# A two-layer graph kernel: masks loaded for two steps at once, fourteen tiles by transfers in the last attention, and two queues and stages rearranged

## The chip, the cores and the metric

The kernel runs on one core of a Trainium2 chip. The time is the device time of one execution in microseconds (us), and less is better. Everything is in fp32, with the exception of the masks, which are bytes.

## What is computed

There are N = 4096 nodes with F = 512 features, in H = 4 heads of D = 128. `adj` is a 0/1 matrix of 4096 x 4096, and both patterns of the first layer are this one matrix, so its two softmaxes are the same. Cut to what matters:

```python
# layer 0: encoder attention, MLP, decoder attention (same weights att), MLP
h   = relu(layernorm(x))
Xw  = einsum('hnd,hde->hne', heads(h), W)
sig = sigmoid(f1[:, :, None] + f2[:, None, :])       # f1, f2: Xw times two vectors
att = where(mask, softmax(where(mask, sig, -inf)), 0)
Xn  = batchnorm(einsum('hij,hjd->hid', att, Xw))
emb = batchnorm(elu(Xn @ Wenc.T + b) + Xn)
Yc  = elu(einsum('hij,hjd,hed->hie', att, heads(emb), W))
x   = x + batchnorm(elu(Yc @ Wdec.T + b) + Yc)
# layer 1: one attention with leaky-relu scores
h     = relu(layernorm(x))
feats = einsum('nf,hfo->hno', h, W1)
attn  = softmax(where(A, leaky_relu(e_self[:, :, None] + e_neigh[:, None, :]), -1e10))
out   = x + relu(einsum('hnm,hmo->hno', attn, feats) + b)
```

## The kernel before

**The three attentions.** The function `attention` (L224 to L564) runs three times: the encoder (L739), the decoder (L846) and the last attention (L1088). Each time it goes through eight blocks, four heads times two halves of 2048 targets (`TB`), and each block through 32 steps. A step handles a tile `e` of 128 sources x 2048 targets. ScalarE fills it (L572 tanh and L573 exp in the encoder and decoder, L1051 in the last attention). VectorE multiplies it by its mask (L574; L1052). Then TensorE accumulates four products of 128 x 128 by 128 x 512 into four banks (L470; in the step `EVICT` = 2 the fourth bank catches up, L467). The decoder handles six pairs of steps with seven products in place of eight (`seven`, L345, and L332). A fifth of the masked tiles is kept in DRAM by the encoder (`ekeep`) and read back by the decoder, which needs no denominators. `weight_tile` (L255) hands out the buffers of `e`: two of one pool and 6, 5 or 7 of another (`ebufs`).

**Denominators.** The encoder and the last attention need the sum of `e` over its sources. Three ways share the 32 tiles of a block, by the tables of L62 to L70, each a pair of `moved` and `by_ones`:

- `moved` tiles are added by the DMA engines, in two transfers of 512 KB each, which GpSimd issues (L490): the first of a block writes the target, the others accumulate. The target is `acc2`, or `w` and `R` in the last attention. The trace names these transfers `acc<-e` and `w<-e`.
- `by_ones` tiles go through TensorE: four products with a stationary of ones of 32 columns, straight into the bank `den` (L268).
- the rest VectorE adds (L498, L500, and L504 for the last six tiles of the last block).

At the end of a block TensorE reduces VectorE's sum with four such products (L517), and the moved sum with four more (L515). A third entry, `ends_later`, puts the latter into step 1 of the following block (L528, seen as `den<-w`). The inner six blocks of the last attention use `GAT`, the outer two `GAT_FIRST` and `GAT_LAST`. In the very last block the products of the last four steps are held back (`late`, L476) until `den` is done, and then L538 and the output follow.

**The end of a block** is spread over the steps of the following one by `ending` (L300): `denominators` copies `den` and writes four rows of it to DRAM (`dens`), `columns` reads them back in another shape (`dcol`), `invert_them` inverts, `inverses` writes them (`rinvs`), and `spread` reads each part back for all partitions (`rb`). The queue of these transfers is `hop` (L263): GpSimd in the encoder and decoder, ScalarE in the last attention. `slack` is 4 steps after encoder block 0, otherwise 0 (L526).

**Masks.** At the start GpSimd issues eight casts of `adjT` from fp32 to bytes, 1024 sources x 2048 targets each (`copy_adjacency`, L600), into DRAM tiles `masks[t][g]` (L166). Every step loads its own mask of 256 KB on SP's queue (L426 to L430, `load_mask` L211) into one of five buffers (L209). The first five are loaded ahead of the encoder (L673). A decoder step whose `e` is read back loads none.

**From the second MLP to the last attention.** `mlp_block` (L747) ends with the product `last_product`. While the statistics of its last feature block are finished, TensorE works on four groups of small products (L903), each followed by a product that serves only to keep it busy (`stay_busy`, L117, which reads `w0Ts`, a table held from the start, L129). `residual` (L866) adds x to a block of 512 nodes: ScalarE scales, VectorE adds. `centred` (L910) takes the mean over features by a product with a constant matrix (`mean_of`; for block 0 it is split into the sum of three feature blocks, L919, and the fourth, L920), subtracts it (L931, four times), and makes relu (`hT`, L935) and squares for the variance (L938 to L940). `values` (L951) multiplies `hT` by the layer's weights, eight products per 128 nodes (L957); `deviation` (L943) gives the scale. Two groups of 128 nodes of block 0 run ahead of it (L964).

**Order.** A scheduler places the instructions of each engine in the order of the program, except where `tc.issue_after` and `pinned` put one behind another, `at(j, ...)` puts work into step j of the following block, and `extras` into named steps.

Of the kernel before, what the change touches and what calls it, by code (L numbers as in the profile page):

```python
# [31 lines left out]
FP = mybir.dt.float32  # L32
U8 = mybir.dt.uint8
# [7 lines left out]
IB = 512  # L41
# [23 lines left out]
ENC = (0, 2, 5, 7, 10, 12, 15, 17, 20, 22, 25), (8, 9, 30, 31)  # L65

GAT_FIRST = (0, 2, 4, 6, 8, 10, 12, 14, 16, 18, 20, 22, 24), (30, 31)
GAT = tuple(range(3, 28, 2)), (31,), True

GAT_LAST = (3, 5, 7, 9, 11, 13, 15, 17, 19, 21, 23), (28, 29, 30, 31)  # L70

# [19 lines left out]
def kernel(ctx, tc, x, xT, adjT, w0, w0T, v0, wencT, wdecT, vecs, w1, w1T, a1, outT):  # L91
# [25 lines left out]
    def stay_busy(behind, n=1, cols=IB):  # L117

        for _ in range(n):
            with tc.issue_after(behind.ins):  # L120
                behind = nc.tensor.matmul(bank()[:, 0:cols], ident, w0Ts.rearrange("p h d -> p (h d)")[:, 0:cols],
                                          start=True, stop=True)
        return behind

# [1 line left out]
    make_identity(nc, ident)  # L126
    ones = consts.tile([P, P], FP, name="ones")
    nc.gpsimd.memset(ones, 1.0)
    w0Ts = consts.tile([P, H, D], FP, name="w0Ts")  # L129
    nc.scalar.dma_start(w0Ts, w0T)  # L130
    vec = consts.tile([P, len(VECS), 4], FP, name="vec")
    nc.scalar.dma_start(vec, vecs)

# [29 lines left out]
    ekeep = [[[dram.tile([P, TB], FP, name=f"ekeep{h}_{t}_{k}") for k in range(NJ // KEEP)] for t in range(NTB)]  # L163
             for h in range(H)]

    masks = [[dram.tile([MG * P, TB], U8, name=f"mask{t}_{g}") for g in range(NJ // MG)] for t in range(NTB)]  # L166

    def everywhere(d, row, lo, n):

# [36 lines left out]
        return nc.sync.dma_start(rowb, everywhere(d, row, 0, TB))  # L206

    def mask_tile(keep):
        return keep.tile([P, TB], U8, name="a", bufs=5)  # L209

    def load_mask(a, tb, j):  # L211

        return nc.sync.dma_start(a, masks[tb][j // MG][(j % MG) * P:(j % MG + 1) * P, :])

    @contextmanager
    def pinned(behind):
# [7 lines left out]
    def attention(what, keep, pools, weights, values, row_of, out, finish, ebufs, modes=None, invert=None,  # L224
# [43 lines left out]
                last_ones = nc.tensor.matmul(den[s * 32:(s + 1) * 32, :], ones[:, 0:32], t[:, s * IB:(s + 1) * IB],  # L268
                                             start=start, stop=stop)

        def denominators(h, tb, den):

            dsb = spool.tile([P, IB], FP, name="dsb", tag="rb", bufs=3)
            (nc.vector.tensor_copy if kept is not None else nc.scalar.copy)(dsb, den)
            hop.dma_start(dens[h][tb], dsb[0:P:32, :])

        def columns(h, tb, dcols):

            dcol = spool.tile([P, TB // P], FP, name="dcol", bufs=2)
            hop.dma_start(dcol, dens[h][tb].rearrange("s (q k) -> (s q) k", k=TB // P))  # L280
            dcols.append(dcol)
# [18 lines left out]
        def ending(h, tb, po, den, slack):  # L300

            outs = [out(spool, h, tb, s, po[s]) for s in range(SB)]
            if den is not None:

                dcols = []
                at(INVERT, denominators, h, tb, den)
                at(INVERT + (0 if hop is nc.gpsimd else 3), columns, h, tb, dcols)
                at(INVERT + slack + (6 if hop is nc.gpsimd else 7), invert_them, dcols)
                at(INVERT + slack + (6 if hop is nc.gpsimd else 10), inverses, h, tb, dcols)
            rbs = {}  # L310
            for s, o in enumerate(outs):
# [84 lines left out]
        for n, (h, tb) in enumerate(blocks):  # L396
# [10 lines left out]
                if tb == 0:  # L407
                    fast[2](h)
            ahead, late = [], []
            adds, held, stores, at_end, next_row = [], [], [], [], None  # L410
            for j in range(NJ):

                with pinned(products_of):
# [9 lines left out]
                if store and kept == "read":  # L423
                    a_load = nc.sync.dma_start(e, ekeep[h][tb][j // KEEP])
                else:
                    if masks0:  # L426
                        a, a_load = masks0.pop(0)
                    else:
                        a = mask_tile(keep)
                        a_load = load_mask(a, tb, j)  # L430

                    with pinned([*(products_of[:1] if kept == "read" and n == 0 and j < 8 else ()),
                                 *(behind if n == 0 and j < EP else ())]):
                        products_of = weights(e, rowb, a, j, h, SB if NJ * n + j < in_parts0 else 1)
# [144 lines left out]
    with tc.tile_pool(name="keep", bufs=1) as keep:  # L579

        with tc.tile_pool(name="f_small", bufs=1) as small, tc.tile_pool(name="f_work", bufs=2) as work:
            xs = []
            w0x = small.tile([P, H, DX], FP, name="w0x")
            v0s = small.tile([P, H, 2], FP, name="v0s")
            nc.scalar.dma_start(v0s, v0)
            nc.scalar.dma_start(w0x[:, :, 0:D], w0)
            for ib in range(NIB):
# [12 lines left out]
            def copy_adjacency(n, behind):  # L600

                t, g = divmod(n, NJ // MG)
                cast = nc.gpsimd.dma_start(masks[t][g], adjT[g * MG * P:(g + 1) * MG * P, t * TB:(t + 1) * TB])
                tc.add_manual_dep(cast.ins, behind.ins.name,
                                  mybir.DependencyInfo(mybir.DependencyClass.Sync, mybir.DependencyReason.DATA),
                                  reason="others first")

            for ib in range(NIB):
# [59 lines left out]
                if ib == SB - 1:  # L668
                    store_rows(rows[0], targets(0))
                    row0 = keep.tile([P, TB], FP, name="rowb", bufs=2)  # L670
                    row0_load = load_row(row0, rows[0], 0)
                    with tc.issue_after(row0_load.ins):
                        masks0 = []  # L673
                        for j in range(5):
                            a = mask_tile(keep)
                            masks0.append((a, load_mask(a, 0, j)))
            store_rows(rows[1], targets(1))
# [100 lines left out]

        with tc.tile_pool(name="m_small", bufs=1) as small, tc.tile_pool(name="m_work", bufs=3) as work:
            yc = [R[3]] + [small.tile([P, N], FP, name=f"yc{o}") for o in range(1, C)]  # L780

            def last_head():
                bn_coefs(stats, "enc_bn_gamma", "enc_bn_beta", a_att, b_att, C - 1, C)
# [67 lines left out]
    v1 = xd  # L851

    edge = ctx.enter_context(tc.tile_pool(name="edge", bufs=1))
    jcol = edge.tile([P, NTB, H, NJ // NTB], FP, name="jcol")
    jcol2 = edge.tile([P, NTB, H, NJ // NTB], FP, name="jcol2")
    nq = edge.tile([P, NTB, H, NJ // NTB], FP, name="nq")
    with tc.tile_pool(name="l_small", bufs=1) as small, tc.tile_pool(name="l_work", bufs=2) as work:
# [5 lines left out]
        a1s = small.tile([P, H, 2], FP, name="a1s")  # L863
        nc.scalar.dma_start(a1s, a1)

        def residual(o, ib):  # L866
            d = nodes(x1[o], ib)
            xt = work.tile([P, IB], FP, name="xt")
            nc.sync.dma_start(xt, xT[o * P:(o + 1) * P, ib * IB:(ib + 1) * IB])
            nc.scalar.activation(d, d, AF.Identity, bias=b_mlp[:, o:o + 1], scale=a_mlp[:, o:o + 1])  # L870
            added = nc.vector.tensor_add(d, d, xt)
            if o == 1:
                nc.gpsimd.tensor_add(S[ib], nodes(x1[0], ib), d)
            elif o == C - 2 or o == C - 1 and ib > 0:
# [20 lines left out]
        for fb in range(C):  # L895
            nc.scalar.dma_start(w1x[:, fb, :, 0:D], w1[fb * P:(fb + 1) * P, :].rearrange("p (h d) -> p h d", d=D))
        pw = bank1()
        last_pe = last_product
        for fb in range(C):
            with tc.issue_after(last_pe.ins):  # L900
                for h in range(H):
                    k = 2 * (fb * H + h)
                    last_pe = nc.tensor.matmul(pw[:, k:k + 2], w1Ts[:, h, fb * P:(fb + 1) * P], a1s[:, h, :],  # L903
                                               start=True, stop=True)
            last_pe = stay_busy(last_pe)
        mean_of = small.tile([P, P], FP, name="mean_of")
        nc.gpsimd.memset(mean_of, 1.0 / F)
        vacc = edge.tile([P, H, D], FP, name="vacc")

        def centred(ib):  # L910

            if ib >= NIB // 2:
                residual(C - 2, ib)
            added = residual(C - 1, ib)
            pm = bank()
            if ib == 0:

                with tc.issue_after(last_pe.ins):
                    nc.tensor.matmul(pm, mean_of, S[ib], start=True, stop=False)  # L919
                nc.tensor.matmul(pm, mean_of, nodes(x1[C - 1], ib), start=False, stop=True)  # L920
                with tc.issue_after(added.ins):
                    nc.vector.tensor_copy(w1x[:, :, :, D:DX],
                                          pw[:, 0:2 * C * H].rearrange("p (c h s) -> p c h s", h=H, s=2))
            else:
                nc.tensor.matmul(pm, mean_of, S[ib], start=True, stop=True)
            hT = work.tile([P, C, IB], FP, name="hT")
            sq = work.tile([P, C, IB], FP, name="sq", bufs=1)

            d = hT if ib else sq
            for fb in range(C):  # L930
                nc.vector.tensor_sub(d[:, fb, :], nodes(x1[fb], ib), pm)  # L931
            for fb in range(C):
                if ib:
                    nc.scalar.activation(sq[:, fb, :], d[:, fb, :], AF.Square)
                last_relu = nc.scalar.activation(hT[:, fb, :], d[:, fb, :], AF.Relu)  # L935
            if ib == 0:
                for fb in range(C):
                    nc.scalar.activation(sq[:, fb, :], d[:, fb, :], AF.Square)  # L938
# [196 lines left out]
```

## Time and profile before

| | us |
|---|---|
| median of three runs | 3187.92 |
| lowest and highest | 3186.09, 3189.45 |
| profiled execution | 3189.23 |
| its span on the core | 3187.4 |
| encoder blocks, start to start on TensorE | 134.5, 126.2, 116.9, 116.4, 118.2, 118.2, 118.1 |
| last product of the second MLP (L724) ends | 2127.76 |
| first product of the values (L957) starts | 2137.93 |
| last attention, blocks start to start on TensorE | 117.2, 111.9, 113.1, 113.1, 113.2, 113.1, 113.1 |
| last attention, block 7 starts | 3066.1 |

| transfer | queue of | count | KB each | us from issue to landing, median |
|---|---|---|---|---|
| `a<-mask` | SP | 720 | 256 | 4.2 |
| `w<-e` | GpSimd | 178 | 512 | 6.5 |
| `acc<-e` | GpSimd | 142 | 512 | 6.9 |
| `mask<-in_adjT` | GpSimd | 8 | 2048 | 107.3 |

The profile is of one execution. Its engines are PE (TensorE), PEld (TensorE's weight loads), DVE (VectorE), ACT (ScalarE), POOL (GpSimd) and SP, the sync engine, which here only issues transfers. The mean clock granted to TensorE was 0.998 of full speed. Times within the execution count from the start of the span; 1.8 us of the execution lie outside it. A line such as `DVE e L574 <- DMA a<-mask: 12.1, 10, 3.0` says that VectorE's instructions of line 574 stood idle for 12.1 us in all, 10 times, 3.0 at most, until the transfer `a<-mask` came in. In the chain of waits a row is a time, a duration and what was running. Fused names such as `R<-R,e` tell the output and the inputs; `acc` lives in a tile of `R` in the last attention.

### The profile page before, as it was taken

Reading aid. Unit: us, or ns where it says so; the run is one execution under the profiler, and the core shown is the slowest. Engines: PE = TensorE matmul, PEld = TensorE weight load, DVE = VectorE, ACT = ScalarE, POOL = GpSimd, SP = SyncE. Lnnn points to the kernel's source line nnn. Section 1 sums busy time; section 2 is a strip of 40 time slices with the busy share of each in tenths; the row PEclk is TensorE's granted clock in tenths of the full one; section 3 lists DMA queues with packets and bytes.
Section 4 is the critical chain, followed back from the end, with each engine's and each line's share of the span. In section 5 each row is a group of like instructions: output and inputs, shape, how many; then the busy total and the mean of one; then the engine's idle time right before and its main releaser. Section 6 shows DMA issues by size and latency. Waiting matters only on the chain.

```text
span 3187.4 us, 30095 instructions
## 1 busy us (share of the span) xinstructions
PE 3140.5 (99%) x10555; PEld 1371.4 (43%) x10555; DVE 2934.3 (92%) x2222; ACT 2572.8 (81%) x1825; POOL 522.3 (16%) x679
## 2 busy tenths in 40 slices
PE   7999999999999999999999999999999999999999
PEld 6334444444444463333333333458644444444444
DVE  7989999999998778999999999785699999999998
ACT  7999999999998449999999999456755666665663
POOL 3001211211211000010100100026312222122221
PEclk9999999999999999999999999999999999999999
DMA  9998978988987014444445454331579999999996
GB/s 212 199 194 252 265 209 232 269 222 228 267 227 205 20 44 149 155 155 159 159 162 165 145 169 145 90 112 57 158 189 232 214 225 237 218 216 236 230 210 174
DMA packets 215488, 590.30 MB, mean 185 GB/s; under 512 B 25928, under 2 KB 29288, under 8 KB 199336
## 3 DMA queue, kind: packets, MB, share of 16 engines
q0 software_dynamic: 70976, 231.94, 38.1%
q1 hardware_dynamic: 132344, 332.53, 30.4%
q10 hardware_dynamic: 12016, 23.90, 2.1%
q8 instruction: 83, 1.36, 0.2%
q14 instruction: 69, 0.57, 0.1%
HBM read 379.20 MB, written 84.30 MB: 145 GB/s over the span
## 4 chain that ended last, share of the span: by engine, by line
PE 73%; DVE 10%; ACT 7%; issue 7%; DMA 2%; DVEq 0%; ACTq 0%; POOL 0%; POOLq 0%
PE ps L470 32%; PE ps L332 22%; PE ps L724 7%; ACT e L572 4%; DVE e L574 4%; PE den L332 3%; PE ps L957 3%; DVE acc L500 3%; ACT e L573 2%; PE den L268 2%; DMA a<-mask 1%; DVE R L500 1%; DVE e L1052 1%; PE ps L806 1%; PE ps L467 1%
## 5 line engine op out<-in xcount | busy, mean ns | idle before, releaser
L470 PE MATMUL ps<-e,R 128*128 128x512 f32 x3992 | 1736.0, 595 | 22.5 <-DVE e L574 18.5
L470 PEld LDWEIGHTS ps<-e,R 128*128 128x128 f32 x3992 | 754.3, 190 | 1000.4 <-issue 924.0
L574 DVE TENSOR_TENSOR e<-e,a 128x2048 f32<-128x2048 f32 (+1 forms) x470 | 1049.6, 2261 | 77.7 <-ACT e L573 64.3
L572 ACT ACTIVATE e<-rowb,score 128x2048 f32<-128x2048 f32 (+1 forms) x470 | 909.0, 1969 | 20.2 <-PE ps L332 9.0
L573 ACT ACTIVATE e<-e 128x2048 f32<-128x2048 f32 (+1 forms) x470 | 866.6, 1879 | 8.3 <-DVE e L574 5.0
L332 PE MATMUL ps<-e,R 128*64 128x512 f32 x2624 | 746.8, 592 | 1.6 <-DVE e L574 1.5
L1051 ACT ACTIVATE e<-rowb,nq,jcol 128x2048 f32<-128x2048 f32 x224 | 459.3, 2088 | 264.1 <-DMA w<-e 137.1
L1052 DVE SCALAR_TENSOR_TENSOR e<-e,jcol,a 128x2048 f32<-128x2048 f32 (+1 forms) x265 | 591.2, 2262 | 2.8 <-ACT e L1051 2.8
L332 PEld LDWEIGHTS ps<-e,R 128*64 128x64 f32 x2624 | 241.9, 137 | 319.8 <-issue 316.2
L500 DVE TENSOR_TENSOR R<-R,e 128x2048 f32<-128x2048 f32 x124 | 282.2, 2276 | 0.0
L500 DVE TENSOR_TENSOR acc<-acc,e 128x2048 f32<-128x2048 f32 x122 | 278.6, 2284 | 1.0
L490 POOL DMA_DIRECT2D w<-e x178 | 149.1, 847 | 610.7 <-DMA w<-e 301.0
L724 PE MATMUL ps<-R,w 128*128 128x512 f32 x512 | 220.8, 592 | 0.6 <-DVE w L698 0.6
L490 POOL DMA_DIRECT2D acc<-e x142 | 119.1, 895 | 517.7 <-DMA acc<-e 199.1
L724 PEld LDWEIGHTS ps<-R,w 128*128 128x128 f32 x512 | 97.1, 190 | 123.0 <-issue 116.5
L332 PE MATMUL den<-e,R 128*64 128x512 f32 x320 | 149.8, 592 | 0.0
L332 PE MATMUL ps<-e,w 128*64 128x512 f32 x288 | 138.1, 592 | 0.7 <-DVE e L574 0.7
L293 POOL DMA_DIRECT2D rb<-rinvs x60 | 34.2, 573 | 519.3 <-DVE R L688 455.2
L957 PE MATMUL ps<-w1x,hT 128*128 128x260 f32 x512 | 115.5, 384 | 1.4 <-ACT hT L935 1.4
L332 PE MATMUL ps<-t,w 128*64 128x512 f32 x336 | 111.2, 592 | 1.0 <-DVE t L341 1.0
L957 PEld LDWEIGHTS ps<-w1x,hT 128*128 128x128 f32 x512 | 96.5, 190 | 19.9 <-issue 3.3
L332 PE MATMUL ps<-t,R 128*64 128x512 f32 x192 | 90.2, 592 | 0.0
(206 smaller groups left out, 2112.9 us busy)
## 6 DMA issues: line engine op xcount, KB each, us to landing
a<-mask SPq DMA_DIRECT2D x720, 256.0 KB, 4.2
w<-e POOLq DMA_DIRECT2D x178, 512.0 KB, 6.5
acc<-e POOLq DMA_DIRECT2D x142, 512.0 KB, 6.9
e<-ekeep SPq DMA_DIRECT2D x48, 1024.0 KB, 5.0
ekeep<-e SPq DMA_DIRECT2D x36, 1024.0 KB, 7.5
mask<-in_adjT POOLq DMA_DIRECT2D x8, 2048.0 KB, 107.3
rowb<-rows SPq DMA_DIRECT2D x16, 1024.0 KB, 7.2
rb<-rinvs POOLq DMA_DIRECT2D x60, 256.0 KB, 4.2
```

The costliest lines, as they stand in the source:

```text
L268: last_ones = nc.tensor.matmul(den[s * 32:(s + 1) * 32, :], ones[:, 0:32], t[:, s * IB:(s + 1) * IB], start=start, stop=stop)
L332: last_half = nc.tensor.matmul(b[g * HD:(g + 1) * HD, :], weight, x, start=start, stop=stop)
L470: last_main = nc.tensor.matmul(b, block(values[h], j), e[:, s * IB:(s + 1) * IB], start=(j == 0), stop=(j == NJ - 1))
L490: nc.gpsimd.dma_start(into_half, e_half, **({"accum_op": ALU.add} if j > moved[0] else {}))
L500: nc.vector.tensor_add(acc, acc, e)
L572: nc.scalar.activation(e, rowb, AF.Tanh, bias=column(score[:, 1], j, h), scale=0.5)
L573: last_act = nc.scalar.activation(e, e, AF.Exp, scale=0.5)
L574: last_dve = nc.vector.tensor_mul(e, e, a)
L724: last = nc.tensor.matmul(z, w[:, fb, o * P:(o + 1) * P], nodes(src[fb], ib), start=(fb == 0), stop=(fb == C - 1))
L957: m = nc.tensor.matmul(banks[k][:, 0:2 * DX], hT[:, fb, c * P:(c + 1) * P], w1x[:, fb, 2 * k:2 * k + 2, :].rearrange("p h x -> p (h x)"), ...
L1051: last_act = nc.scalar.activation(e, rowb, AF.Relu, bias=column(nq, j, h), scale=column(jcol, j, h))
L1052: last_dve = nc.vector.scalar_tensor_tensor(e, e, column(jcol2, j, h), a, ALU.add, ALU.mult)
```

## The change

**The last attention's tables.** The inner blocks add the 14 odd tiles 3 to 29 by transfers and none by ones; before it was the 13 odd tiles 3 to 27, with tile 31 by ones. The two outer blocks stay.

**Masks.** Two steps share one transfer. The DRAM tiles are laid out with a partition's eight rows side by side, and the casts write them so. A buffer holds two steps' masks and there are three, six steps in all (before: five). Three pairs are loaded ahead of the encoder. In a whole run there are 384 transfers of 512 KB for 720 of 256 KB. The decoder now loads both masks of a pair of which it uses one.

**Denominators of encoder block 0.** `dens` and `dcol`, the first two transfers of that block's end, are issued on SP's queue, not on GpSimd's, and `columns` comes two steps later. All other blocks and transfers stay as they are.

**Values in parts.** For block 0 the scale, the addition of x, the product of L920, the subtractions and relu are made for 128 columns first, then for the other 384. The product of L919 moves up to where the first of the four `stay_busy` products was.

**w0Ts.** It is no longer held throughout, but loaded twice, for the first stage and for the first MLP. `stay_busy` reads a tile `filler` instead, which GpSimd sets to ones.

The diff, cut to its core:

```diff
@@ tables
 GAT_FIRST = (0, 2, 4, 6, 8, 10, 12, 14, 16, 18, 20, 22, 24), (30, 31)
-GAT = tuple(range(3, 28, 2)), (31,), True
+GAT = tuple(range(3, 30, 2)), (), True
@@ stay_busy
-                behind = nc.tensor.matmul(bank()[:, 0:cols], ident, w0Ts.rearrange("p h d -> p (h d)")[:, 0:cols],
+                behind = nc.tensor.matmul(bank()[:, 0:cols], ident, filler[:, 0:cols],
@@ w0Ts, called in the first stage and at the head of the first MLP
-    w0Ts = consts.tile([P, H, D], FP, name="w0Ts")
-    nc.scalar.dma_start(w0Ts, w0T)
+    def load_w0T(pool):
+        w0Ts = pool.tile([P, H, D], FP, name="w0Ts")
+        nc.scalar.dma_start(w0Ts, w0T)
+        return w0Ts
@@ masks
-    masks = [[dram.tile([MG * P, TB], U8, name=f"mask{t}_{g}") for g in range(NJ // MG)] for t in range(NTB)]
+    masks = [[dram.tile([P, MG * TB], U8, name=f"mask{t}_{g}") for g in range(NJ // MG)] for t in range(NTB)]
...
-        return keep.tile([P, TB], U8, name="a", bufs=5)
+        return keep.tile([P, 2 * TB], U8, name="a", bufs=3)
...
-        return nc.sync.dma_start(a, masks[tb][j // MG][(j % MG) * P:(j % MG + 1) * P, :])
+        k = j % MG // 2
+        return nc.sync.dma_start(a, masks[tb][j // MG][:, k * 2 * TB:(k + 1) * 2 * TB])
@@ attention, ending
-                at(INVERT, denominators, h, tb, den)
-                at(INVERT + (0 if hop is nc.gpsimd else 3), columns, h, tb, dcols)
+                at(INVERT, denominators, h, tb, den, nc.sync if slack else hop)
+                at(INVERT + (0 if hop is nc.gpsimd else 3) + slack // 2, columns, h, tb, dcols, nc.sync if slack else hop)
@@ attention, step j
-                    if masks0:
-                        a, a_load = masks0.pop(0)
-                    else:
-                        a = mask_tile(keep)
-                        a_load = load_mask(a, tb, j)
+                    if two_masks[0] != j // 2:
+                        if masks0:
+                            two, a_load = masks0.pop(0)
+                        else:
+                            two = mask_tile(keep)
+                            a_load = load_mask(two, tb, j)
+                        two_masks = j // 2, two
+                    a = two_masks[1][:, j % 2 * TB:(j % 2 + 1) * TB]
@@ copy_adjacency
-                cast = nc.gpsimd.dma_start(masks[t][g], adjT[g * MG * P:(g + 1) * MG * P, t * TB:(t + 1) * TB])
+                rows_of = adjT[g * MG * P:(g + 1) * MG * P, t * TB:(t + 1) * TB]
+                cast = nc.gpsimd.dma_start(masks[t][g].rearrange("p (m i) -> p m i", i=TB),
+                                           rows_of.rearrange("(m p) i -> p m i", p=P))
@@ first masks
-                        for j in range(5):
+                        for j in range(0, 6, 2):
@@ the edge pool
+    filler = edge.tile([P, IB], FP, name="filler")
+    nc.gpsimd.memset(filler, 1.0)
@@ residual
-        def residual(o, ib):
+        def residual(o, ib, parts=(slice(0, IB),)):
...
-            nc.scalar.activation(d, d, AF.Identity, bias=b_mlp[:, o:o + 1], scale=a_mlp[:, o:o + 1])
-            added = nc.vector.tensor_add(d, d, xt)
+            for p in parts:
+                nc.scalar.activation(d[:, p], d[:, p], AF.Identity, bias=b_mlp[:, o:o + 1], scale=a_mlp[:, o:o + 1])
+                added = nc.vector.tensor_add(d[:, p], d[:, p], xt[:, p])
@@ small products behind the second MLP
+        pm0 = bank()
...
-            last_pe = stay_busy(last_pe)
...
+            if fb == 0:
+                with tc.issue_after(last_pe.ins):
+                    last_pe = nc.tensor.matmul(pm0, mean_of, S[0], start=True, stop=False)
+            else:
+                last_pe = stay_busy(last_pe)
@@ centred
-            added = residual(C - 1, ib)
-            pm = bank()
+            parts = (slice(0, IB),) if ib else (slice(0, P), slice(P, IB))
+            added = residual(C - 1, ib, parts)
             if ib == 0:
+                pm = pm0
                 with tc.issue_after(last_pe.ins):
-                    nc.tensor.matmul(pm, mean_of, S[ib], start=True, stop=False)
-                nc.tensor.matmul(pm, mean_of, nodes(x1[C - 1], ib), start=False, stop=True)
+                    for p in parts:
+                        nc.tensor.matmul(pm[:, p], mean_of, nodes(x1[C - 1], ib)[:, p], start=False,
+                                         stop=(p.stop == IB))
...
-            for fb in range(C):
-                nc.vector.tensor_sub(d[:, fb, :], nodes(x1[fb], ib), pm)
-            for fb in range(C):
-                if ib:
-                    nc.scalar.activation(sq[:, fb, :], d[:, fb, :], AF.Square)
-                last_relu = nc.scalar.activation(hT[:, fb, :], d[:, fb, :], AF.Relu)
+            for p in parts:
+                for fb in range(C):
+                    nc.vector.tensor_sub(d[:, fb, p], nodes(x1[fb], ib)[:, p], pm[:, p])
+                for fb in range(C):
+                    if ib:
+                        nc.scalar.activation(sq[:, fb, :], d[:, fb, :], AF.Square)
+                    last_relu = nc.scalar.activation(hT[:, fb, p], d[:, fb, p], AF.Relu)
```

More of the change, by code (lines that the diff above doesn't have):

```diff
@@ L269, in add_to_den, with denominators @@
                                              start=start, stop=stop)
-        def denominators(h, tb, den):
+        def denominators(h, tb, den, hop):
             dsb = spool.tile([P, IB], FP, name="dsb", tag="rb", bufs=3)
@@ L275, in denominators, with columns @@
             hop.dma_start(dens[h][tb], dsb[0:P:32, :])
-        def columns(h, tb, dcols):
+        def columns(h, tb, dcols, hop):
             dcol = spool.tile([P, TB // P], FP, name="dcol", bufs=2)
@@ L409, in attention @@
             ahead, late = [], []
-            adds, held, stores, at_end, next_row = [], [], [], [], None
+            adds, held, stores, at_end, next_row, two_masks = [], [], [], [], None, (None, None)
             for j in range(NJ):
@@ L584 @@
             v0s = small.tile([P, H, 2], FP, name="v0s")
+            w0Ts = load_w0T(small)
             nc.scalar.dma_start(v0s, v0)
@@ L780 @@
             yc = [R[3]] + [small.tile([P, N], FP, name=f"yc{o}") for o in range(1, C)]
+            w0Ts = load_w0T(small)
             def last_head():
@@ L897 @@
         pw = bank1()
+        pm0 = bank()
+        mean_of = small.tile([P, P], FP, name="mean_of")
+        nc.gpsimd.memset(mean_of, 1.0 / F)
         last_pe = last_product
@@ L904 @@
                                                start=True, stop=True)
-            last_pe = stay_busy(last_pe)
-        mean_of = small.tile([P, P], FP, name="mean_of")
-        nc.gpsimd.memset(mean_of, 1.0 / F)
+            if fb == 0:
[3 more added lines that the diff above has]
+                last_pe = stay_busy(last_pe)
         vacc = edge.tile([P, H, D], FP, name="vacc")
@@ L924, in centred @@
             else:
+                pm = bank()
                 nc.tensor.matmul(pm, mean_of, S[ib], start=True, stop=True)
```

## The prediction

> **What bounds the kernel now.** I read the page first: engines, then the chain. TensorE is busy almost throughout, so the page alone can't say what a microsecond is worth in a stage; VectorE and ScalarE are near full too.
>
> ```profile
> PE 3140.5 (99%) x10555; PEld 1371.4 (43%) x10555; DVE 2934.3 (92%) x2222; ACT 2572.8 (81%) x1825; POOL 522.3 (16%) x679
> ...
> PE 73%; DVE 10%; ACT 7%; issue 7%; DMA 2%; DVEq 0%; ACTq 0%; POOL 0%; POOLq 0%
> ```
>
> So I asked for stretches of one attention block each (columns: window, length, busy PE, PEld, DVE, ACT, POOL, clock, DMA share, GB/s). Encoder blocks 0, 1 and 4, then two inner blocks of the last attention:
>
> ```profile
> 64.50:199.00 134.50, 123.28 (x344) 49.77 (x344) 123.33 (x60) 133.34 (x73) 0.00 (x0) 1.00 1.05 193
> 199.00:325.20 126.20, 122.39 (x340) 50.68 (x336) 118.07 (x67) 119.71 (x66) 16.04 (x22) 0.99 0.92 225
> ...
> 558.50:676.70 118.20, 116.57 (x309) 49.51 (x305) 114.35 (x64) 118.20 (x65) 22.30 (x30) 1.00 0.90 240
> ...
> 2498.75:2611.86 113.11, 113.11 (x284) 49.05 (x288) 113.11 (x56) 71.55 (x43) 25.28 (x30) 1.00 0.95 224
> 2611.86:2724.97 113.11, 113.11 (x284) 49.05 (x288) 113.11 (x56) 72.38 (x43) 25.23 (x30) 1.00 0.96 225
> ```
>
> Three things are to be seen. In the encoder ScalarE is the engine without a gap: from block 2 on its busy time is the block's length. Its two activations start 1.893 and 1.800 us apart, 32 x 3.693 = 118.2 us, which is block 4. Only blocks 0 and 1 have ScalarE idle. In the last attention PE and DVE both have no gap in six blocks. And DMA is at 0.95 there, 1.05 in block 0, where the eight casts of the adjacency run.
>
> Waits within 64 to 330 us, and the chain of the same stretch:
>
> ```profile
> POOL dcol L280 <- DMA dens<-dsb: 37.3, 1, 37.3
> ...
> DVE e L574 <- DMA a<-mask: 12.1, 10, 3.0
> ACT e L573 <- DVE e L574: 5.0, 3, 3.1
> ...
> DVE dcol L284 <- DMA dcol<-dens: 2.9, 1, 2.9
> ACT e L572 <- PE den L268: 2.5, 3, 1.1
> ```
>
> ```profile
> 146.06 21.29 DMA a<-mask
> ...
> 207.22 37.32 issue
> 244.56 3.08 DMA dcol<-dens
> ```
>
> Masks and the first block's denominators hold VectorE up, and through the e buffers ScalarE: 5.0 + 2.5 = 7.5 us of ScalarE idle, all that the encoder has.
>
> The end of the last attention, VectorE above, TensorE below; and the chain where the values begin:
>
> ```profile
> 3161.53 4.60 DVE L504 TENSOR_TENSOR R<-R,e 128x2048 f32<-128x2048 f32 x2
> 3167.92 1.04 PE L268 MATMUL den<-R,ones 128*32 128x512 f32 x8
> ```
>
> ```profile
> 2135.63 0.87 PE ps L920 x2
> 2136.53 0.70 DVE sq L931
> 2137.25 0.64 ACT hT L935
> 2137.93 7.31 PE ps L957 x32
> ```
>
> VectorE's last add ends at 3166.13, TensorE wants the sum at 3167.92: 1.79 us of slack, no more.
>
> [...] from 100 to 180 us there are 2402 mask packets (2048 B, 96 ns) beside 2818 cast packets (322 ns). [...] GpSimd issued `dens` at 206.6 us and it landed at 244.3, just after the last cast (243.9). [...] four ones products take 0.93 us, while one main product takes 0.858. [...]
>
> **Part 1, ones out (L68).** Removed: four products of tile 31 in each of the six inner blocks. Two rows of den products (x16) take 1.85 us, so 0.93 each: 6 x 0.93 = 5.5 us of TensorE. VectorE's work is unchanged: 13 moved + 1 by ones before, 14 moved now, 18 tiles (17 adds) either way; tile 29 leaves its adds and 31 enters. VectorE in an inner block, by distance of starts: 32 x 2.263 + 17 x 2.202 + 4 x 0.602 + 0.24 = 112.5 us; TensorE 113.11, now 112.18. The trace gives TensorE a lead to eat: e was ready 3.6 us ahead at its least in block 1, growing 0.7 per block; now it shrinks 0.2 to 0.3 per block, to about 2.3, so no stall within blocks. But in the last block VectorE has the last word: it has no gap from 2285 to 3166, so its last add stays at 3166.13 after the stage's start, and TensorE's product of R can move only from 3167.92 to 3166.2. **Worth 1.7 us, not 5.5**; 3.8 us come back as a wait on L504. Bounds: 5.5 if VectorE got faster somewhere, 0 if a transfer delays it.
>
> Moved in: six tiles of two 512 KB accumulations. The 13th tile's last half landed at 2609.0, 2720.4, ... 3056.2, and TensorE reads w (L528's `den<-w`) at 2616.4, 2729.5, ... 3068.9. The 14th takes some 5.6 us more (its e was ready at 2595, so only the earlier half's landing holds it). Landing about 2614.6, 2726 against 2614.6, 2726.8 (TensorE earlier by 0.93 per block). A wait of up to a microsecond in an early block eats from the 3.8 that TensorE has to spare: 0. Queued behind it on GpSimd: `out<-R` and the next block's first accumulation, which wait for `den<-w` now (14 us). ScalarE finishes e 4 us or more ahead of VectorE throughout, so late buffers have that cover.
>
> **Part 2, two masks in one transfer.** 720 transfers of 256 KB become 384 of 512 KB; packets of 4096 B. From 96 ns at 2048 B and 328 at 8192 B I estimate 173, twice 96 is the other end. Under the casts an engine gives a mask 8 packets x (322 + 96) = 3.3 us at best; counted, 18.8 loads in 80 us, 4.26 us each, where ScalarE wants one per 3.69. Now 8 x (322 + 190) = 4.1 us for two steps. The waits of VectorE on masks (12.1 us) should go. Lookahead stays: the third buffer is free four steps ahead, as the fifth was. In the last attention bytes are equal; engine time falls by 0 to 3 us of 26 per block, against 256 x 326 ns / 16 = 5.2 us added. Decoder: 48 x 256 KB more, at a DMA share of 0.44 to 0.49: nothing. First mask of the last attention: landed at 2267.65, used at 2268.9; 512 KB lands some 0.7 later: 0 to 0.3. Casts write the same 2048 B runs, only spread: 0.
>
> **Part 3, denominators of encoder block 0 on SP.** `dens` and `dcol` no longer stand behind the casts; VectorE's wait of 2.9 (L284) goes, and GpSimd's accumulations needn't queue behind a 37 us wait. Added waits on SP: `dens` for L274, `dcol` for `dens`. Behind them on SP is the mask pair of steps 10 and 11, which VectorE wants some 16 us later. A quiet queue lands such a transfer in 3 to 4 us (`dcol<-dens`, 3.5): no stall. Had it the 15 to 17 us that masks took here, it would be one.
>
> Parts 2 and 3 together: ScalarE's 7.5 us of idle. TensorE has 119.8 and 119.1 us of work in blocks 0 and 1 (128 x 0.858, and 10 ones tiles) against ScalarE's 118.2, and eight e buffers take up the 2.5 us difference and the start. What may stay: the e of step 12 is held until its accumulation gets through behind the casts. Ends 2 and 7.5; **I take 6.0**.
>
> **Part 4, values in parts.** L919 takes a filler's place earlier: -0.93 ahead of the pair. Then 128 columns suffice to begin: x by 0.2 us less at least, L920 0.22 for 0.87, [...] L935 0.27 (as L987) for 0.57. From the last product at 2127.76: 4 x 0.79 + 0.86 + 3 x 0.96 = 2134.7, + 0.4 + 0.2 + 0.3, first value at 2135.7 instead of 2137.93: 2.2. Squares end about 1.1 us earlier (2140.5), S by 2143.0, when the two blocks of values end too. Ends 1.0 and 2.3; **I take 2.1**. If ScalarE's eight small activations take longer than thought, it is late for the second block of values, and 1 us goes.
>
> **Other.** Second `w0Ts` load: ACT issues it after 1042.7; its table load then has until 1049.9, 5.9 us of cover; 0.3 if it waited for L688's last. Filler memset: GpSimd is 16% busy. 0.
>
> **Sum:** 6.0 + 2.1 + 1.7 = 9.8 us. The profiled execution took 3189.23 (span 3187.4, 1.8 around it), 1.3 above the median of 3187.92: 3179.4 by it, 3178.1 by the median. I forecast **3178**. A measurement of this kernel tells about 0.2% (6.4 us) from no change: faster is below 3181.5, slower above 3194.3.
>
> **Rivals.** (B) The encoder's gain is mostly hidden: accumulations behind the casts (244 us) still hold e, 1.5 instead of 6.0: **3182.5**. For it: 0.92 DMA share in block 1; against: the chain names masks and dens, not `acc<-e`. (C) Ones worth their full 5.5: **3174**; against it, VectorE's gapless row. (D) Slower: the accumulations become the bound of the last attention. First issue to last landing is 102.6 us for 13 tiles (2617.8 to 2720.4), 108.2 for 14, and 1.4 from `den<-w` to the next issue: 109.6 of VectorE's 112.4. From 0.2 us more per tile on (7.9 now), blocks stretch; at 5% more (0.4 us), 14 x 0.4 - 2.8 = 2.8 x 6 = 17 us, less the 8 gained elsewhere: **3197**. For it: 0.957 + 5.2/113 = 1.00 DMA share; against: block 0 had 1.05, and mask packets halve. (E) SP stands 15 us behind `dens`, and VectorE waits some 7 us: **3185**.
>
> **Chances:** main 0.55, B 0.20, C 0.10, D 0.08, E 0.07. Faster: nearly all of the main case, C, and under half of B, 0.71; slower D, 0.08; within 0.2% the rest, 0.21. Range 3174 (C) to 3185 (E); outside lie D and a few tails. The main case alone: 3175.5 to 3181.
>
> **What would show it.** Right: no ScalarE gap over 0.5 us from 64 to 325; `dens` landing within 5 us; blocks 0 and 1 together 6 us shorter; values beginning 2 us sooner; in the last attention VectorE still gapless, and a new PE wait of 3 to 4 us on L504 at the end. Wrong: VectorE gaps in the last attention, ACT waits on `w<-e` reaching VectorE, or PE waits at `den<-w` adding to more than 4 us.

## The result, and the profile after

The changed kernel takes 3196.15 us (median of 8 runs, 3190.78 to 3203.5), the kernel before 3187.89 in the same runs (3186.02 to 3189.45): a ratio of 1.0026, with a 95% interval from 1.0018 to 1.0035. It is slower by 8.3 us, where I forecast 9.8 us less. The runs of the changed kernel also lie further apart, 12.7 us against 3.4. Its profiled execution took 3193.98 (span 3192.2), 2.2 below its median, and the one of before 1.3 above; so the two traces are 4.8 us apart, not 8.3, and what follows from them is said of these two executions.

The page: engines, the chain that ended last, and transfers (queue, count, KB each, median us from issue to landing).

```profile
PE 3138.2 (98%) x10507; PEld 1369.8 (43%) x10507; DVE 2933.6 (92%) x2227; ACT 2573.8 (81%) x1830; POOL 530.4 (17%) x690
...
PE 52%; DVE 16%; issue 14%; DMA 11%; ACT 6%; POOL 1%; DVEq 0%; ACTq 0%; SPq 0%; POOLq 0%
...
a<-mask SPq DMA_DIRECT2D x384, 512.0 KB, 5.1
w<-e POOLq DMA_DIRECT2D x190, 512.0 KB, 7.2
acc<-e POOLq DMA_DIRECT2D x142, 512.0 KB, 7.6
```

PE, DVE and ACT have as much work as before, within 2.3 us. What is new is DMA in the chain, 11% for 2%. And the accumulations, which the diff doesn't touch, take longer to land: 7.2 for 6.5 us (`w<-e`), 7.6 for 6.9 (`acc<-e`).

The same stretches as before, of the changed kernel: encoder blocks 0, 1 and 4, then inner blocks 2 to 4 of the last attention (all by VectorE's starts).

```profile
63.20:185.70 122.50, 116.74 (x310) 48.15 (x311) 118.48 (x58) 122.37 (x68) 0.00 (x0) 0.99 1.05 195
185.70:311.00 125.30, 120.06 (x329) 49.84 (x328) 114.67 (x64) 123.88 (x68) 14.28 (x19) 1.00 0.99 235
545.50:665.90 120.40, 116.83 (x304) 49.43 (x304) 114.51 (x64) 118.55 (x65) 22.11 (x29) 1.00 0.87 236
2485.60:2598.30 112.70, 109.31 (x260) 47.05 (x259) 112.43 (x57) 70.52 (x41) 26.72 (x32) 0.98 0.99 233
2598.30:2713.40 115.10, 115.10 (x280) 50.01 (x279) 112.45 (x56) 70.54 (x41) 26.70 (x32) 1.00 0.97 228
2713.40:2829.90 116.50, 112.27 (x265) 48.11 (x264) 112.48 (x56) 70.84 (x41) 26.75 (x32) 0.97 0.97 227
```

(Columns as in the prediction.) By VectorE's starts, encoder blocks 0 and 1 took 128.4 and 124.6 us before and take 122.5 and 125.3. Block 4 took 118.2 and takes 120.4: a new loss. In the last attention the blocks were 112.4 apart; blocks 2 to 5 now take 112.7, 115.1, 116.5 and 115.7, with VectorE's work 112.4 to 112.5. From the first mask product of that stage to the last it was 892.7 us and is 902.6. That is a loss of 9.9 us.

The chain through it (start, duration, what ran), and two waits of the inner blocks (in all, times, longest):

```profile
2486.35 7.01 DMA w<-e
...
2493.65 7.34 DMA w<-e
...
2501.03 1.07 PE den L272 x4
...
2508.22 103.00 PE ps L477 x240
2611.22 1.04 PE den L272 x8
...
2612.28 0.04 DVE R L505
```

```profile
PE den L272 <- DMA w<-e: 7.6, 4, 2.8
...
DVE R L505 <- PE den L272: 5.9, 2, 3.3
```

Block 1's last accumulation lands at 2501.0. TensorE had wanted `w` since 2496.6 and stood idle for 3.4 us in two pieces. By the prediction's sum it has 112.18 us of work per block for VectorE's 112.4, so it catches up hardly at all. A block later its reduction of `R` comes 2.65 us too late for VectorE's first sum, which overwrites `R` (L505). So VectorE, which sets the pace of the stage, waits. The same happened two blocks later (TensorE 4.2 us, VectorE 3.3), and in between VectorE lost 4.0 us on an `e` that came late: ScalarE's queue stood 5.3 us behind the issue of `dcol`, for `dens`, which follows TensorE's late product of `w`. VectorE's waits, 2.65 + 4.0 + 3.3, are the 9.9 us.

### The profile page after: what moved, and what is told of

Same layout as the page of the kernel before. It is cut to its first block, busy times and chain, and to the rows that moved or that the text cites. A ratio compares the mean times of both kernels' runs of the same rounds, so it can differ in the third digit from the quotient of the medians.

```text
span 3192.2 us, 29192 instructions
## 1 busy us (share of the span) xinstructions
PE 3138.2 (98%) x10507; PEld 1369.8 (43%) x10507; DVE 2933.6 (92%) x2227; ACT 2573.8 (81%) x1830; POOL 530.4 (17%) x690
## 4 chain that ended last, share of the span: by engine, by line
PE 52%; DVE 16%; issue 14%; DMA 11%; ACT 6%; POOL 1%; DVEq 0%; ACTq 0%; SPq 0%; POOLq 0%
PE ps L336 22%; PE ps L477 13%; PE ps L734 6%; DVE e L1074 5%; DMA acc<-e 4%; DMA w<-e 4%; DVE R L507 4%; ACT e L579 3%; PE den L336 3%; PE ps L979 3%; DVE e L581 3%; DVE acc L507 2%; ACT e L580 2%; DMA rinvs<-dcol 1%; PE ps L817 1%
## 5 line engine op out<-in xcount | busy, mean ns | idle before, releaser
L497 POOL DMA_DIRECT2D w<-e x190 | 158.5, 843 | 608.4 <-DMA w<-e 364.8
L336 PE MATMUL ps<-t,w 128*64 128x512 f32 x336 | 111.3, 592 | 1.1 <-DVE t L345 1.1
```

The lines of the kernel that those rows point to most:

```text
L336: last_half = nc.tensor.matmul(b[g * HD:(g + 1) * HD, :], weight, x, start=start, stop=stop)
L497: nc.gpsimd.dma_start(into_half, e_half, **({"accum_op": ALU.add} if j > moved[0] else {}))
```

## The experiments

There were two theories at first. **A**: the fourteenth tile makes the chain of accumulations longer than VectorE's block (rival D of the prediction). **B**: the mask pairs slow the accumulations. The expectations after the first four runs split B: **P**, the longer packets; **U**, two masks at once (bunching); **L**, the layout in DRAM. "Before" is the kernel before, timed beside the run.

| kernel | median | before | ratio, 95% interval |
|---|---|---|---|
| changed | 3196.15 | 3187.89 | 1.0026, 1.0018 to 1.0035 |
| e1 changed, old table | 3190.83 | 3187.89 | 1.0009, 1.0001 to 1.0018 |
| e2 only table | 3185.78 | 3187.89 | 0.9993, 0.9985 to 1.0001 |
| e3 only pairs | 3194.98 | 3187.89 | 1.0023, 1.0014 to 1.0032 |
| e4 ones left out | 3186.49 | 3187.89 | 0.9993, 0.9985 to 1.0001 |
| e5 pairs by two loads | 3194.43 | 3187.52 | 1.0021, 1.0012 to 1.0029 |
| e6 pairs in a row | 3240.92 | 3187.52 | 1.0168, 1.0154 to 1.0182 |
| e7 only layout | 3188.03 | 3187.22 | 1.0001, 0.9993 to 1.0009 |
| e8 only denominators | 3194.21 | 3187.52 | 1.0020, 1.0012 to 1.0028 |
| e9 only values | 3185.27 | 3187.22 | 0.9994, 0.9987 to 1.0000 |
| e10 changed, single masks | 3190.73 | 3187.52 | 1.0012, 1.0005 to 1.0018 |
| e11 pairs first, then single | 3182.29 | 3187.22 | 0.9985, 0.9977 to 0.9992 |
| e12 pairs in a row again | 3225.72 | 3187.40 | 1.0120, 1.0106 to 1.0133 |
| e13 pairs in the encoder | 3186.05 | 3187.40 | 0.9996, 0.9988 to 1.0004 |

### Which part costs: e1 to e4

e1 is the changed kernel with the old line 68.

> The changed kernel with the last attention's old table (13 tiles by transfers, tile 31 by ones). Theory A, the fourteenth tile makes the chain of accumulations longer than VectorE's 112.4 us per block: the stall of the last attention is gone, VectorE's blocks 112.4 us apart again, and the gains before it stay (4.6 us up to the end of the second MLP, 1.5 in the values): 3181 to 3183 us. Theory B, the mask pairs slow the accumulations: blocks 3 to 5 of the last attention still take 114 to 116 us, 3190 us or more.

e2 is the kernel before with the new line 68.

> The kernel before with the new table alone (14 tiles by transfers, none by ones, single masks). Theory A: the last attention loses 8 to 14 us as in the changed kernel, 3196 to 3202 us. Theory B: accumulations keep their pace of 7.9 us per tile, 3186 to 3188 us.

e3 has the hunks on masks, casts and `w0Ts` alone.

> The kernel before with mask pairs alone (three buffers of two, casts and first loads to match, the table w0Ts moved to make room). Theory A: some of the encoder's gain, nothing lost later, 3183 to 3187 us. Theory B: the encoder gains as much, but the last attention's accumulations slow down and it loses 5 us or more, 3190 to 3195 us.

e4 keeps 13 transfers and leaves tile 31 of the inner blocks out of the sum:

```diff
-                        held.append(e)
+                        held.extend([] if ends_later else [e])
```

> The kernel before, but tile 31 of the six inner blocks of the last attention is left out of the denominators: no ones products and no transfer in their place. By the prediction's step (VectorE sets the end, 1.79 us of slack) 5.5 us less TensorE work give 1.7 us, 3186.2 us, with a new wait of TensorE on L504 at the end. The rival, TensorE sets the pace of every block: 5.5 us, 3182.4 us.

Theory A falls as it stood: the table alone (e2) doesn't cost, its point estimate is 2.1 us less. e1 has the blocks of theory A, 112.4 us apart, and the time of theory B. e3 is 7.1 us slower, as B had it, but not where I had put it: with 13 tiles its last attention keeps its 112.4 us too, and it loses its time in the encoder. Both causes are needed in the last attention, as the time from the first issue of an inner block to its last landing shows:

| | block 1 | 2 | 3 | 4 | 5 | 6 |
|---|---|---|---|---|---|---|
| before, 13 tiles, single | 106.1 | 104.3 | 102.6 | 101.8 | 100.7 | 99.1 |
| e1, 13 tiles, pairs | 108.1 | 107.3 | 106.9 | 103.5 | 104.2 | 103.2 |
| e2, 14 tiles, single | 110.8 | 112.8 | 109.6 | 107.5 | 107.9 | 107.2 |
| changed, 14 tiles, pairs | 116.2 | 114.0 | 116.2 | 114.3 | 108.7 | 111.3 |

The next block's accumulations start only after TensorE has read `w`, about 1.4 us after. With 112.4 us for a block, about 111 is the limit. e2 stays at or under it but for one block, where TensorE waited 0.65 us. The changed kernel goes well past it four times, and waited at two of them. On top of e1 the new table costs 5.3 us; on the kernel before it takes 2.1 off.

e4 tests the step "worth 1.7 us, not 5.5". It came out at 1.4, and its interval (0.3 slower to 4.8 faster) leaves out the 5.5. The wait that I had named is there, 2.6 us for the 3 to 4 expected (TensorE, with the idle time before it in brackets):

```profile
3162.89 1.94 PE L268 MATMUL den<-R,ones 128*32 128x512 f32 x8 [2.60 <-DVE R L504]
```

### Why pairs slow the accumulations: e5, e6, e7, e12

e5 loads a pair by two transfers, from the old layout, so with the old packets:

```diff
-        return nc.sync.dma_start(a, masks[tb][j // MG][:, k * 2 * TB:(k + 1) * 2 * TB])
+        for m in range(2):
+            load = nc.sync.dma_start(a[:, m * TB:(m + 1) * TB], masks[tb][j // MG][(2 * k + m) * P:(2 * k + m + 1) * P, :])
+        return load
```

> Mask pairs alone, but each pair loaded by two transfers of 256 KB issued together, with the DRAM layout and the 2048 B packets of before. The accumulations land 6.2 us after issue before and 6.5 to 6.8 with pairs. Theory P, the longer packets hold the accumulations' packets up: 6.2 us again, 3187 to 3190 us. Theory U, two steps' masks at once are the trouble, whatever their packets: 6.5 us or more, and 3194 us or more. Theory L, the layout in DRAM (rows at a stride of 16 KB): as P.

e6 and e12 keep one transfer in 4096 B packets, but lay each pair out in one piece (`[MG // 2 * P, 2 * TB]`), with four casts per group in e6, two in e12:

> Mask pairs alone, one transfer of 512 KB in packets of 4096 B, but each pair contiguous in DRAM (4096 B rows, one after the other; each cast is issued as four). Theory L, the stride of 16 KB is the trouble: accumulations land in 6.2 us, 3184 to 3188 us. Theories P and U: 6.5 us or more, 3193 to 3197 us as with pairs alone.

> Mask pairs alone, one transfer of 512 KB in packets of 4096 B, each pair contiguous in DRAM, with two casts per group and those of the second half of the targets issued after the first stage, so that the encoder should start at about 64 us again. Theory P, the length of the packets is enough: accumulations land in 6.5 us or more and encoder blocks 3 to 7 lose 3 to 6 us together; whole time 3192 to 3197 us if the start isn't late. Theory L, the stride has to come with it: blocks 3 to 7 lose less than 1 us, 3185 to 3189 us.

e7 changes only the layout:

> The kernel before, single masks in 256 KB transfers, only the layout in DRAM changed to the new one (a partition's eight mask rows side by side, so that one mask is 128 rows of 2048 B at a stride of 16 KB) with the casts to match. Theory L, the stride slows the masks and what runs beside them: accumulations land in 6.4 us or more after issue (6.2 before), encoder blocks 3 to 7 lose 2 us or more together, 3190 us or more. Theory P, it is the length of the packets or the bunching of the two masks: 3186 to 3189 us.

The "6.2 us" of these texts is a mean from the end of the issue. Below are the median and the mean from the start of the issue, for encoder blocks 3 to 7 (440 to 1010 us) and the inner blocks of the last attention (2400 to 3050); e6 and e12 by 50 and 36 us later. Beside them stand ScalarE's waits on accumulations, and the time of encoder blocks 3 to 7 together, from VectorE's first mask product to the end of its last (all in us).

| masks there | kernel | encoder: landing, median | mean | ScalarE's waits | blocks 3 to 7 | last attention: landing, median | mean |
|---|---|---|---|---|---|---|---|
| short packets | before, e2, e4, e7 to e11 | 6.7 to 6.9 | 7.1 to 7.2 | 0 to 0.4 | 589.3 to 589.8 | 6.7 to 7.0 | 7.0 to 7.2 |
| short, two at once | e5 | 6.9 | 7.3 | 0 | 589.4 | 6.6 | 7.2 |
| long, in a row | e6, e12 | 7.1, 7.4 | 7.4, 7.4 | 0.4, 1.5 | 589.8, 590.2 | 7.0, 7.1 | 7.3, 7.3 |
| long, at a stride | e1, e3, changed | 7.1 to 7.6 | 7.5 to 7.7 | 3.7 to 4.7 | 592.4 to 594.6 | 7.2 to 7.4 | 7.4 |

Two masks at once don't do it, and the stride with short packets doesn't (e7 is the kernel before within its interval). So P is right that no loss is seen without long packets. That their length is enough is not shown: in a row, the accumulations come later by about half as much, and encoder blocks 3 to 7 lose less than 1 us, which e12's text had set as the outcome of theory L. A loss of 3 us and more is seen only with long packets at a stride. What the stride adds stays open.

The whole times of e6 and e12 say nothing on the pairs, since both kernels started late, at 122 and 91 us for 64: GpSimd, which issues the casts between its share of the first stage, stood idle for 105.7 us in e6 until earlier casts had landed.

The packets allow an estimate. From 2400 to 3050 us a mask packet took 97.9 ns on average before and takes 199.5, the accumulations' packet 331 and 325; the masks' share of the engines is 22.3% in both. The accumulations' 153 transfers of 512 KB before are 19500 packets of 4096 B in that stretch, so about 128 each, 8 for each of the 16 engines on average. If each of these waits for one mask packet at most, 0.10 us more now, the transfer lands at most 8 x 0.10 = 0.8 us later; at a stride it lands 0.2 to 0.6 later on average. That they wait so is my assumption: no run here shows the order of the packets on one engine. And the length can't be all of it, since the mask packets of e6 and e12 are about as long (196.5 and 191.3 ns).

e5 met the number of theory U, 3194, for another reason: its encoder blocks 3 to 7 and its last attention have no loss, its decoder takes 939.4 us for 929.5. VectorE there waits 20.3 us for kept tiles (`e<-ekeep`), which are loaded on the same queue as the masks (1.5 before, 9.7 in the changed kernel, whose decoder takes 929.8). Why the waits grow so in e5 stays open.

### The denominators and the values: e8, e9, e10

> The kernel before with the denominators of encoder block 0 on SP's queue alone. By the prediction's step the wait of 2.9 us on dcol and what stands behind dens on GpSimd goes: ScalarE's idle time from 230 to 290 us falls by 2 to 4 us, 3184 to 3186 us. Rival E: SP's masks stand behind dens, 3190 us or more.

> The kernel before with the values in parts alone. From the last product of the second MLP to the first product of the values 8.0 to 8.6 us instead of 10.1, and 3185.8 to 3186.5 us. If the last attention's start takes it back: 3187.5 us.

> The changed kernel with the single masks of before: new table, denominators of encoder block 0 on SP, values in parts. If the parts add up: 2.1 from the table, 2 to 3 from the denominators, 1.5 from the values, 3181 to 3183 us. If one of them rests on the pairs: 3185 us or more.

With single masks the denominators on SP cost 6.7 us: rival E, to its size. Here are SP's queue in e8, and VectorE's and ScalarE's waits of 195 to 300 us:

```profile
197.10 11.35 SPq L213 DMA_DIRECT2D a<-mask  x4
208.79 0.62 SPq L275 DMA_DIRECT2D dens<-dsb  x1
224.90 0.32 SPq L280 DMA_DIRECT2D dcol<-dens  x1
225.32 13.26 SPq L213 DMA_DIRECT2D a<-mask  x6
```

```profile
DVE e L574 <- DMA a<-mask: 14.0, 5, 8.3
...
ACT e L573 <- DVE e L574: 8.4, 1, 8.4
```

`dens` was issued behind four masks, beside the casts, and SP could issue `dcol` only 16.1 us later. The masks behind `dcol` were issued only then, and VectorE stood 8.3 us for one of them. With pairs (changed kernel) `dens` was issued at 197.7 and `dcol` at 205.5, 7.8 later, and no mask was late. Pairs alone (e3), on the other hand, bring VectorE to `dcol` sooner, and it waits 10.4 us for it. Encoder blocks 0 and 1 took 253.0 us in the profiled execution of before, but 250.4 to 251.0 in those of e2, e4, e7 and e9, whose encoder is that of before (in e7 with the other layout of the masks). Against these, e3 takes 251.5, e8 256.2, and the changed kernel 247.9. So neither half gains alone, the denominators on SP even cost 5 to 6 us, and together they gain about 3.

e10 isn't 3181 to 3183 because of that 8.3 us wait, which is in it too: 6.7 for e8, less 2.1 for e2 and 1.9 for e9, is 2.7, and it is 3.2 us slower. It also has the fourteen tiles with single masks in the five old buffers, and its last attention takes 893.2 us, so the loss there goes with the pairs. e9 is 1.9 us faster (0 to 4 by its interval).

### What each place is worth: e11 and e13

e11 keeps everything but uses pairs only in encoder blocks 0 and 1, from one buffer of six masks (`ring`), and single masks of 256 KB after; e13 has pairs in all encoder blocks (without the `n < 2`).

```diff
+                    if loaded == used:
+                        k = 2 if what == "enc" and n < 2 else 1
...
+                        a_load = load_mask(ring, used, tb, j, k)
+                        loaded += k
+                    a = ring[:, used % 6 * TB:(used % 6 + 1) * TB]
```

> The changed kernel, but pairs only in encoder blocks 0 and 1, where the casts run, and single masks after (six slots of one ring buffer; new layout in DRAM; new table, denominators on SP and values in parts kept). Theory P, the pairs cost through their packets: the gain of 5 us in blocks 0 and 1 stays, the losses of blocks 3 to 7 and of the last attention go, 3178 to 3181 us. Theory L: the losses stay in part, 3185 us or more.

> As the kernel with pairs first (3182.3 us), but pairs in all eight encoder blocks; single masks in the decoder and the last attention. If the pairs cost in the encoder as well as in the last attention: ScalarE waits for accumulations again in blocks 2 to 7, 3 to 6 us in all, the last attention keeps its 112.4 us per block: 3185 to 3188 us. If it was the last attention alone: 3182 us.

e11 is faster than both kernels: 4.9 us less than before, 2.5 to 7.3 by its interval. Its 3182.3 lies above the 3178 to 3181 of theory P, since the gain in blocks 0 and 1 is about 3 us and not 5. Each against its own runs of the kernel before, e13 is 3.6 us above e11, and the changed kernel 9.6 above e13. So pairs cost about 3.6 us in encoder blocks 2 to 7; the intervals of the two runs, put together, allow from nothing to 7, but the traces agree (blocks 3 to 7 take 594.1 us for 589.3). They cost 9.6 in what follows, where the traces put all of it in the last attention (902.6 against 892.7 us; the decoder 929.8 and 929.5). With the 4.9 gained in e11 this makes up the change, by construction. e13 shows both speeds in one execution, accumulations of encoder blocks 3 to 7 with pairs:

```profile
who waited for it (us, times):
  POOL acc L499: 192.7, 56
  ACT e L581: 4.8, 7
...
DMA to landing us min/median/max: 2.9/7.6/12.3
```

In its last attention, with single masks, the median is 6.7. In e11, ScalarE doesn't wait for an accumulation in these encoder blocks at all.

## Why the prediction was wrong, by its own steps

**Part 1** was right in mechanism, and its size fits: 1.7 us, and e2 and e4 gave 2.1 and 1.4, though their intervals reach from no change to 4.8. The traces are sharper: from VectorE's first mask product of the stage to the start of TensorE's products of `R` at the end it is 899.0 us before and 897.3 in e2, e4, e11 and e13. One term was too small: the fourteenth tile took 6.9 us more per block in e2, not 5.6. Rival D had the mechanism of the loss: accumulations that stretch the blocks "from 0.2 us more per tile on". By D's own measure, first issue to last landing, a tile took 7.88 us before, 7.84 in e11 (14 tiles, single masks) and 8.10 in the changed kernel. I gave D one chance in twelve because I saw its cause in the tile alone. That D's 3197 lies near the measured time is in part luck: it had 17 us lost in the last attention and 8 gained elsewhere.

**Part 2 is the step that failed**: "In the last attention bytes are equal; engine time falls by 0 to 3 us of 26 per block". I priced the masks' own packets. Their time didn't fall (22.3% of the engines before and after), and I set nothing for the accumulations that share the engines with them. For a mask behind the casts I had reckoned with one cast packet to each of its own (8 x (322 + 96) ns, an estimate; from 100 to 180 us the trace of before has 2818 beside 2402), but I made no such estimate for an accumulation behind the masks. It lands 0.2 to 0.6 us later on average, which is ScalarE's wait in the encoder (4.8 us in e13, none in e11) and TensorE's in the last attention (7.6 us at `w`; with what VectorE then waits, the stage is 9.9 us longer). Two of the signs that I had named for being wrong came: gaps of VectorE in the last attention, and waits at `den<-w` of more than 4 us. Under the casts the step held: packets of 172 ns for the 173 estimated, and no wait on a mask up to 330 us.

**Part 3** held only together with part 2. I expected `dens` in 3 to 4 us; it was 7.8 to the issue of `dcol`, which landed 9.1 later.

**Parts 2 and 3 together were mis-sized**, 6.0. ScalarE's idle of 7.5 us in blocks 0 and 1 was that of one execution. In the profiled executions of e2, e4, e7 and e9, it is 4.9 to 5.7; the wait on `dcol`, 2.9 before, is 0.7 to 0.9. Of e7:

```profile
ACT e L573 <- DVE e L574: 2.9, 3, 1.3
ACT e L572 <- PE den L268: 2.7, 3, 1.2
DVE dcol L284 <- DMA dcol<-dens: 0.9, 1, 0.9
```

And of the changed kernel, the same stretch:

```profile
ACT e L579 <- PE den L272: 1.1, 1, 1.1
ACT e L579 <- DMA acc<-e: 0.9, 1, 0.9
ACT e L580 <- ACT e L579: 0.4, 1, 0.4
```

So the term is about 5.3 - 2.4 = 2.9 us, and the blocks' times above say about 3.

**Part 4**: 10.17 us from the last product to the first values before, 8.60 after and 8.59 in e9. That is 1.6 for the 2.1 taken, inside its ends. The chain shows the missing piece:

```profile
2129.26 0.96 PE ps L121 x2
2130.23 0.88 PE ps L939 x4
...
2131.14 0.30 DVE sq L953
...
2131.46 0.32 ACT hT L957
```

I let the subtraction start after the product of 128 columns, 0.22 us, which is also its time in this trace, from start to start. It starts after both products, 0.88: the 0.66 between them accounts for the difference. The 0.2 us that my sum has for the subtraction was an estimate of mine; the four of 128 columns start 0.20 us apart. (My sum also had a slip: 2134.7 + 0.4 + 0.2 + 0.3 is 2135.6, not 2135.7.)

At the end of the changed kernel the wait on VectorE's last sum isn't there: VectorE ends its sum at 3170.7, TensorE reaches `R` at 3172.4, late from its own stalls. In e11, which has no such stalls, it is there, 1.40 us for the 3 to 4 expected.

With the sizes measured, the gains are 2.9 + 1.6 + 1.7 = 6.2 us, which e11 fits (4.9, 2.5 to 7.3).

What stays open: why long packets at a stride cost more than long packets in a row, and what slows e5's decoder.

## What to carry to other kernels

Here a change to the packets of one queue lengthened another's transfers, while in the last attention the share of the engines that the changed packets took stayed at 22.3%. With mask packets of 4096 B at a stride, for 2048 B, the accumulations landed 0.2 to 0.6 us later on average, and 0.1 to 0.3 later where the rows lay one after the other in DRAM. Look at the transfers beside the one that you change, and at who waits for them. A chain of dependent transfers that just fits into its block has to be priced with a margin, since two edits that each fit can break it together. Before a wait is priced as a gain, look whether it is the same in other executions, and ask of two edits that each lift a wait whether either is worth anything alone.

## What the runs showed that I had not expected

- A transfer of 8 KB on SP's queue, behind four masks under the casts, held the queue for 16.1 us (e8), and for 7.8 us behind a pair's load.
- With 32 or 16 casts issued by GpSimd in place of 8, the encoder started some 58 and 27 us later (e6, e12). In e6 GpSimd waited at 24 of the 32 until earlier ones had landed; whether the chip or the program's own semaphores ask for that isn't shown.
- The dependence of a subtraction on a product of 128 columns was met only at the end of the next product into the same bank (0.88 us for 0.22). Whether the chip or the program's dependences ask for that isn't shown.
